# Attention tiles of a four-layer convolution kernel: the order of the two head pairs' score matmuls

## The chip, the cores and the metric

The kernel runs on one core of one Trainium2 chip. The metric is the device time of one execution in microseconds (us); where several runs were made, their median is given. The core's engines run their own instruction streams and wait for each other through semaphores: TensorE (PE, with its weight loads listed apart as PEld), VectorE (DVE), ScalarE (ACT), GpSimd (POOL) and SyncE (SP), which here issues DMAs.

## The reference

The input x is 4 x 256 x 48 x 48. Four layers follow, each adding to x what it computes from the group-normalised x:

```python
x = x + _L0_conv_ref(_gn(x), ...)   # 7x7 dilated conv, softmax over 49 taps, weighted patches
x = x + _L1_conv_ref(_gn(x), ...)   # 3x3 conv, sign weights
x = x + _L2_conv_ref(_gn(x), ...)   # 3x3 conv, ternary weights
x = x + _L3_conv_ref(_gn(x), ...)   # windowed linear attention
```

The change lies in layer 3. With 8 heads of 32 channels:

```python
q = sigmoid(Wq x);  k = sigmoid(Wk x);  v = Wv x / |Wv x|      # per head
for w in (1, 2, 4):                                            # window 48/w
    wk  = box sum of k over the window around each pixel
    wkv = box sum of the outer products k v over the same window
    attn = (q . wkv) / (q . wk + 1e-6)
out = Wout [attn of the three windows] + bout
```

## The kernel before, in words

Layers 0 to 2 come first (in the profiled execution up to 1389 us) and the change does not touch them.

Layer 3 does not form the box sums of k v. It works like masked attention without a softmax: for a block of queries (8 image rows of 48 pixels, of one image and one half of the heads) and a tile of 128 keys (8 rows by 16 columns) it computes the scores k . q, sets those outside the window to zero, and sums v over the keys with the masked scores as weights. `Block` (from line 1826) holds one block of queries; there are 48 blocks (4 images, 2 halves with 4 heads each, 6 row groups) with 15 key tiles on average, 720 tiles in all. A tile's work in TensorE's program is:

- `scores` (line 1837), called once for each pair of heads (`pr` = 0 or 1). It takes a tile of the pool `ps_s`, two PSUM banks, and issues two matmuls of 32 rows by 128 columns, one for each head of the pair. The four heads of a half lie in partitions 0, 32, 64 and 96, so the first pair's matmuls use TensorE's row groups 0 and 32, the second pair's 64 and 96. In f32 each matmul is two passes, and leaves two records in the profile.
- `unseen` (line 1855): one small bf16 matmul for each head, in the same row groups and banks, adds -1024 to scores that the widest window does not see. It goes through the first pair, then the second.
- `masked` (line 1875) is the work of other engines on the banks. In a full tile (all its rows inside the widest window) ACT applies Relu to the second pair, DVE multiplies the first pair by the middle window's mask, then ACT does the first pair and DVE the second. In an edge tile ACT does the first pair and DVE the second, once each. POOL makes the narrowest window's part from the middle's. The results are `sm` tiles in SBUF.
- `sums` (line 1980): matmuls of v (128 rows by 32 columns, a column group for each head) with the `sm` tiles into three accumulators `acc`. The main loop (line 2201) places the sums of a tile two tiles behind its scores (`LAG = 2`), after the scores and penalties of the present tile.

`ps_s` has two tiles, one for each pair, so that a tile's scores start when ACT and DVE have left the banks of the tile before. PSUM is full: four banks of scores, three accumulators and one bank for all other products.

All these engines are wrapped in `InOrder` (line 200): their instructions stay in the order in which Python issues them. Between tiles `advance` (line 302, called at 2229) lets jobs put in a step each: projections of the next image, key sums, norms, window states, the output projection. Their pace is set by an estimate of each tile's mask and sum times; it does not depend on the order of the pairs.

The lines that this document follows are the main loop's call

```python
ss = [blocks[i].scores(pr, a, c) for pr in range(NPR)]
blocks[i].unseen(ss, a, c)
ahead.append(blocks[i].masked(a, c, ss))
```

with NPR = 2, and the two matmul loops in `scores` and `unseen`. Every instruction carries the line of the wrapper, L208, in the profile, so groups are told apart by the names of their tiles: s (scores and penalties), sm, acc.

Of the kernel before, what the change touches and what calls it, by code (L numbers as in the profile page):

```python
# [211 lines left out]
def conv_preact_kernel(  # L212
# [89 lines left out]
    def advance(time=None):  # L302

        nonlocal step, spare
        step += 1
        spare = ALL if time is None else min(spare, 0.0) + time
        for entry in list(active):
            if entry[0] <= step:
                wait = next(entry[1], None)
                if wait is None:  # L310
                    active.remove(entry)
                else:
                    entry[0] = step + wait
# [4 lines left out]
    def until(*keys):  # L318
        while not made.issuperset(keys):
            assert active  # L320
            advance()
# [1246 lines left out]
    with (  # L1568
# [23 lines left out]
        NPR = HG // 2  # L1592
# [406 lines left out]
        def seen(wi, a, rb):  # L1999
            r0, r1 = rows_seen(wi, a, rb)  # L2000
            return r0 < r1
# [128 lines left out]
        def begun(i):  # L2130

            b, ct, rb = order[i]
            if (ct, rb) == (0, 0) and b + 1 < B:
                everything = ("q0", "q1", "k0", "k1", "v")
                following = Projection(b + 1, scr, *bank_m).groups([(a, everything) for a in range(NRB)])
                start(paced(following, 2))
            blocks[i] = Block(b, ct, rb, qs.pop(i))

        def midway(i):

            b, ct, rb = order[i]
            if (b, ct) == (0, 0) and 0 < rb <= NRB - seen_first:
                a = seen_first - 1 + rb
                until(("k", 0, 0, a), ("v", 0, a))
                load_kv(0, 0, a)
            if ct == NCT - 1:
                start(prepare(i))
            if i + 1 < len(order):
                start(window_state(i + 1))
                nb, nct, nrb = order[i + 1]  # L2150
                until(("q", nb, nct, nrb))
                qs[i + 1] = load_q(*order[i + 1])

        def done(i):

            b, ct, rb = order[i]
            finishing.append((i, blocks.pop(i).stage))
            nb, nct = b + (ct + 1) // NCT, (ct + 1) % NCT
            if nb < B:
                for a in LOADS.get(rb, ()):  # L2160
                    until(("k", nb, nct, a), ("v", nb, a))
                    load_kv(nb, nct, a)
# [7 lines left out]
        def mask_time(i, a, c):  # L2170

            rb = order[i][2]

            def elements(wi, cols):
                y0, y1 = rows_seen(wi, a, rb)
                return 2 * (y1 - y0) * (cols[1] - cols[0])

            if not rows_whole(a, rb):
                return 150 + 0.87 * elements(0, cols_seen(0, c))
            on_act = sum(150 + 0.87 * elements(0, cols) for cols in strips(c))  # L2180
            on_dve = (elements(1, cols_seen(1, c)) + 130) / 0.96
            return on_act + on_dve + max(0, max(on_act, on_dve) - min(on_act, on_dve))

        def sums_time(i, a, c, at):

            rb, time = order[i][2], 0
            for wi in range(NW):
                if seen(wi, a, rb):
                    y0, y1 = rows_seen(wi, a, rb)
                    parts = strips(c) if wi == 0 and rows_whole(a, rb) else [cols_seen(wi, c)]  # L2190
                    time += product_time((y1 - y0) * sum(p1 - p0 for p0, p1 in parts))
            if at == 0:
                time += 300
            if at == 6:
                time += product_time(sum(RB * (c1 - c0) for c0, c1 in map(cols_whole, range(NKC))))
            return time

        blocks, ahead = {}, []
        start(window_state(0))
        start(finish_all())  # L2200
        for n in range(len(stream) + LAG):
            if n < len(stream):
                i, a, c, at, last = stream[n]
                if at == 0:
                    begun(i)
                ss = [blocks[i].scores(pr, a, c) for pr in range(NPR)]
                blocks[i].unseen(ss, a, c)
                ahead.append(blocks[i].masked(a, c, ss))
                if at == 5:
                    midway(i)  # L2210
            if n >= LAG:
                i, a, c, at, last = stream[n - LAG]
                sms = ahead.pop(0)
                if at == 0:
                    if i >= 2:
                        until(("done", i - 2))
                    blocks[i].begin()
                if at == 6:
                    until(("window", i))
                    blocks[i].whole(i)  # L2220
                for wi in (1, 0, 2):
                    if seen(wi, a, order[i][2]):
                        blocks[i].sums(wi, a, c, sms)
                if last:
                    done(i)
            time = 1000.0
            if LAG <= n < len(stream):
                time = 900.0 + mask_time(*stream[n][:3]) - sums_time(*stream[n - LAG][:4])
            advance(max(time, 500.0))
# [46 lines left out]
```

## Time and profile before

| what | value |
|---|---|
| median of 3 runs | 3482.7 us (3479.43 to 3486.44) |
| profiled execution: device time, span | 3485.36 us, 3483.6 us |
| granted TensorE clock, mean | 0.951 |
| span before layer 3's tiles, PE busy in it | 1389 us, 1162.9 us |
| span of layer 3's tiles, PE busy in it | 2095 us, 1896.7 us |
| in it, busy on s: PE, PEld | 719.2 us, 264.4 us |
| in it, busy on sm from s: DVE, ACT | 753.0 us, 559.1 us |
| in it, POOL busy (all work) | 1353.8 us |

The page lists an engine's busy time, the chain of work that ended last with its shares of the span, and groups of like instructions: output<-inputs, count, busy time, mean length of one in ns, and the idle time of the engine before them with what ended most of it. An answer on waits reads: who waited for whom, us in total, number of times, longest. A timeline line has the start and the length in us, the engine, the operation, the operands and how many instructions are merged in it; for merged lines the length is from the first start to the last end. Busy time of a group of concurrent matmuls is counted once, while the mean length is that of one.

### The profile page before, as it was taken

What the parts mean: (1) busy time and instruction counts of PE and PEld (TensorE: products, weight loads), DVE (VectorE), ACT (ScalarE), POOL (GpSimd) and SP (SyncE); (2) the same over time, 40 slices, a digit from 0 to 9 for tenths busy, and PEclk for the clock granted to TensorE, in tenths of its full rate; (3) what the DMA queues carried; (4) which work ended last, traced back from release to release, by engine and by line L of the source; (5) the groups of instructions that cost most, each with busy time, mean ns of one, the idle gap of its engine ahead of it and who ended that gap; (6) DMA issues with size and microseconds to landing.
All of it is one profiled execution on the core that took longest, in us unless ns stands there. A gap on an engine that the chain in (4) does not pass through costs nothing.

```text
span 3483.6 us, 78045 instructions
## 1 busy us (share of the span) xinstructions
PE 3059.6 (88%) x31634; PEld 1931.6 (55%) x31634; DVE 1994.0 (57%) x3595; ACT 1041.5 (30%) x2782; POOL 1532.2 (44%) x2548
## 2 busy tenths in 40 slices
PE   3579999999899788888789988889998999989998
PEld 2467776767768557444344544444554444545544
DVE  7986488568657336465564445554456554444444
ACT  0012111211111423444323433433344433334432
POOL 0000030021011214587886678786557786534443
PEclk9799899999999899999899999999999999999999
DMA  7745413413322422344554444354423454401221
GB/s 256 236 139 174 141 63 122 154 54 129 120 94 85 138 89 98 120 132 145 164 144 129 127 137 146 116 158 134 124 81 119 130 150 122 114 29 52 81 63 56
DMA packets 373052, 423.34 MB, mean 122 GB/s; under 512 B 129076, under 2 KB 328532, under 8 KB 371540
## 3 DMA queue, kind: packets, MB, share of 16 engines
q1 hardware_dynamic: 371491, 416.32, 38.3%
q8 instruction: 249, 4.08, 0.5%
q0 software_dynamic: 144, 1.24, 0.2%
q14 instruction: 112, 0.91, 0.1%
q10 hardware_dynamic: 1056, 0.79, 0.1%
HBM read 288.24 MB, written 131.25 MB: 120 GB/s over the span
## 4 chain that ended last, share of the span: by engine, by line
PE 56%; POOL 12%; DVE 11%; ACT 4%; issue 3%; DMA 3%; SPq 1%; ACTq 0%; POOLq 0%; DVEq 0%
PE s L208 15%; PE cv L208 14%; PE acc L208 11%; PE out_ps L208 6%; PE proj_ps L208 4%; DVE sm L208 3%; POOL nhi L208 3%; ACT sm L208 3%; POOL sm L208 3%; POOL pt L208 2%; PE ap L208 2%; POOL vu L208 1%; DVE l2v L208 1%; DVE v L208 1%; DVE k L208 1%
## 5 line engine op out<-in xcount | busy, mean ns | idle before, releaser
L208 DVE TENSOR_TENSOR sm<-s,masks 128x432 f32<-128x432 f32 (+8 forms) x1152 | 634.4, 578 | 627.8 <-PE s L208 582.0
L208 POOL TENSOR_TENSOR sm<-sm,masks 128x336 f32<-128x336 f32 (+8 forms) x768 | 606.1, 809 | 662.6 <-DVE sm L208 656.2
L208 ACT ACTIVATE sm<-s 128x128 f32<-128x128 f32 (+3 forms) x1680 | 559.1, 361 | 1030.9 <-PE s L208 820.9
L208 PE MATMUL s<-qs,ks 32*128 32x320 f32 (+3 forms) x5760 | 664.5, 506 | 127.9 <-DVE sm L208 61.6
L208 PE MATMUL acc<-sm,vs 128*32 128x64 f32 (+13 forms) x14976 | 681.8, 306 | 48.6 <-POOL sm L208 48.5
L208 PE MATMUL cv<-vx,wt 128*128 128x288 f32 x2080 | 560.1, 425 | 93.2 <-DVE vx L208 52.6
L208 PEld LDWEIGHTS acc<-sm,vs 128*32 128x32 f32 x14976 | 347.9, 110 | 384.5 <-issue 258.4
L208 PEld LDWEIGHTS cv<-vx,wt 128*128 128x128 f32 x2080 | 402.5, 198 | 214.5 <-issue 56.7
L208 PEld LDWEIGHTS s<-qs,ks 32*128 32x128 f32 x5760 | 264.4, 187 | 422.9 <-ACT sm L208 172.4
L208 POOL MEMSET v<- 128x16 f32 (+1 forms) x120 | 18.5, 215 | 727.7 <-DVE vx L208 634.5
L208 PE MATMUL cv<-v,wl 128*128 128x384 f32 x1152 | 225.1, 355 | 25.7 <-DVE x L208 10.6
L208 DVE TENSOR_SCALAR sm<-s 128x672 f32<-128x672 f32 (+1 forms) x144 | 118.6, 824 | 202.8 <-PE s L208 198.1
L208 PEld LDWEIGHTS cv<-v,wl 128*128 128x128 f32 x1152 | 214.3, 194 | 36.0 <-issue 15.9
L208 PE MATMUL s<-masks 24*128 24x128 bf16 (+4 forms) x2880 | 217.7, 236 | 0.0
L208 POOL TENSOR_TENSOR pt<-pt 128x144 f32<-128x144 f32 x336 | 188.5, 561 | 23.0
L208 POOL TENSOR_TENSOR v<-l2v,v 128x384 fp32r<-128x384 f32 x96 | 109.0, 1163 | 120.2 <-ACT v L208 111.3
L208 POOL TENSOR_TENSOR nhi<-nhi,nq 128x384 f32<-128x384 f32 x144 | 144.8, 1033 | 0.2
L208 PE MATMUL cv<-pad,wl 128*128 128x384 bf16 x864 | 143.1, 327 | 0.0
L208 PE MATMUL out_ps<-o,wout_sb 128*128 128x384 f32 x288 | 130.2, 534 | 3.6 <-DVE res L208 2.8
L208 PEld LDWEIGHTS <-masks 24*128 24x128 bf16 x2880 | 101.5, 95 | 53.9 <-issue 3.5
L208 PEld LDWEIGHTS <-wl 128*128 128x128 bf16 x864 | 83.8, 97 | 59.3 <-issue 0.7
L208 PE MATMUL out_ps<-stage,wout_sb 128*128 128x384 f32 x288 | 116.4, 486 | 0.0
(176 smaller groups left out, 3568.6 us busy)
## 6 DMA issues: line engine op xcount, KB each, us to landing
wt<-wt SPq DMA_DIRECT2D x48, 768.0 KB
kb_d<-pt SPq DMA_DIRECT2D x48, 576.0 KB
rc<-r_d SPq DMA_DIRECT2D x192, 144.0 KB
nhi<-kb_d SPq DMA_DIRECT2D x120, 192.0 KB
nlo<-kb_d SPq DMA_DIRECT2D x88, 192.0 KB
o_d<-stage SPq DMA_DIRECT2D x24, 576.0 KB
o<-o_d SPq DMA_DIRECT2D x24, 576.0 KB
wl<-wl_d SPq DMA_DIRECT2D x16, 768.0 KB
```

The lines of the kernel that those rows point to most:

```text
L208: return lambda *args, **kwargs: self.tc.keep_in_program_order(op(*args, **kwargs))
```

## The change

The first and the second pair's scores change places in TensorE's program. `reversed(range(NPR))` allocates and computes pair 1 first, then pair 0; the `[::-1]` puts the two tiles back in their old order in `ss`, so that `unseen` and `masked` treat them as before: penalties for pair 0, then pair 1, and the same operations of ACT and DVE on each.

```diff
@@ -2203,7 +2203,7 @@
                 i, a, c, at, last = stream[n]
                 if at == 0:
                     begun(i)
-                ss = [blocks[i].scores(pr, a, c) for pr in range(NPR)]
+                ss = [blocks[i].scores(pr, a, c) for pr in reversed(range(NPR))][::-1]
                 blocks[i].unseen(ss, a, c)
                 ahead.append(blocks[i].masked(a, c, ss))
                 if at == 5:
```

## The prediction

> **What bounds the kernel now.** I read the page first (busy time, chain, groups), then the waits and the chain of layer 3's stretch, then single tiles in the timeline.
>
> ```profile
> PE 3059.6 (88%) x31634; PEld 1931.6 (55%) x31634; DVE 1994.0 (57%) x3595; ACT 1041.5 (30%) x2782; POOL 1532.2 (44%) x2548
> PE s L208 15%; PE cv L208 14%; PE acc L208 11%; PE out_ps L208 6%; PE proj_ps L208 4%; DVE sm L208 3%; POOL nhi L208 3%; ACT sm L208 3%; POOL sm L208 3%; POOL pt L208 2%; PE ap L208 2%; POOL vu L208 1%; DVE l2v L208 1%; DVE v L208 1%; DVE k L208 1%
> L208 PE MATMUL s<-qs,ks 32*128 32x320 f32 (+3 forms) x5760 | 664.5, 506 | 127.9 <-DVE sm L208 61.6
> L208 PE MATMUL s<-masks 24*128 24x128 bf16 (+4 forms) x2880 | 217.7, 236 | 0.0
> ```
>
> TensorE is busy 88% of the span, and the scores (s) are the largest item of the chain that ended last. 5760 score records are 720 tiles of 8: four heads, two passes each. 5760 times 506 ns would be 2915 us, but their busy time is 664.5: the four heads run side by side in four groups of 32 rows. Within layer 3 alone (1389 to 3484 us) the chain's answer gives PE s 25.7% of 2095 us, 538 us, the largest item again. The waits of that stretch:
>
> ```profile
> DVE sm L208 <- PE s L208: 780.1, 617, 11.0
> PE s L208 <- DVE sm L208: 61.6, 92, 9.5
> PE s L208 <- ACT sm L208: 60.4, 110, 4.0
> ```
>
> TensorE itself waits for a released score bank only some 122 us in all. The individual records show 272 of 720 tiles starting after such a gap. So two kinds of tile matter: those where TensorE arrives late anyway (448), and those where the masks of the tile before hold it (272). Two tiles from the timeline:
>
> ```profile
> 2507.91 0.93 PE L208 MATMUL s<-qs,ks 32*128 32x384 f32 x8
> 2508.66 0.24 PE L208 MATMUL s<-masks 24*128 24x128 bf16 x4
> 2508.93 0.81 DVE L208 TENSOR_TENSOR sm<-s,masks 128x624 f32<-128x624 f32 x1 [2.14 <-PE s L208]
> ...
> 2501.47 0.96 PE L208 MATMUL s<-qs,ks 32*128 32x320 f32 x8
> 2502.11 0.38 PE L208 MATMUL s<-masks 24*128 24x128 bf16 x4
> 2502.41 0.75 PEld L208 LDWEIGHTS acc<-sm,vs 128*32 128x32 f32 x24 [0.32 <-issue]
> 2502.49 1.12 DVE L208 TENSOR_TENSOR sm<-s,masks 128x432 f32<-128x432 f32 x2 [0.46 <-PE s L208]
> ```
>
> In the first, all four heads start together. In the second, pair two's bank came free 0.155 us late, so its scores and its penalty matmuls follow by that much: the block of four penalty matmuls is 0.38 long instead of 0.24. Yet DVE, which needs the first pair alone, starts at 2502.49, at the end of the whole block, as in the first tile.
>
> **What the skill says.** The Trainium skill, "TensorE: Matmul & The Clock Gate", Part 3, says that matmuls in different row groups run concurrently and start about 4 ns apart, and that matmuls are strict FIFO in start and end. The trace has the concurrency, at 6.7 ns spacing. On FIFO it is mixed: a head's second pass starts 0.373 us after its first, and the next head's first pass, later in the program, starts after 0.007; if the two passes count as one instruction the rule holds. That DVE waits for the block's end supports ends in order: pair one's completion is reported only after pair two's scores, which stand before it. "TensorEngine Tiling (Array Packing)", Key Properties, says that changing the tiling mode drains the array: here the first sum (128x32) starts 0.145 us after the last 128-column penalty matmul starts and 0.225 to 0.25 after one of 320 to 384 columns, so the last penalty matmul sets when the sums begin.
>
> **The change, part by part.**
>
> 1. Instructions. None is added or removed. In the built program 2880 TensorE instructions change their row position and their bank: per tile the four score matmuls go from row groups 0, 32, 64, 96 to 64, 96, 0, 32. The penalty matmuls stay at 0, 32, 64, 96. No DMA moves, and no instruction of DVE, ACT, POOL or SP.
>
> 2. Waits. Every engine's waits stand at the same places with the same values. The pool hands the slot that is released first to whichever pair is allocated first; so the first two score matmuls still wait for what the first two waited for. The change therefore doesn't let either pair start on another release. Cost nothing; there is no cover to lose.
>
> 3. Pair one's scores start two issue places later: 2 x 6.7 = 13.4 ns where both banks are free. The penalty matmuls begin with its row group 0. The records of an undisturbed tile have the penalties at 0.643, 0.649, 0.656 and 0.663 us after the first score, each as its row group comes free. After the change row group 0 comes free at 0.656; in order the four stand at 0.656, 0.663, 0.669 and 0.676. The block ends 13.4 ns later, and so do the sums and everything behind. 720 x 13.4 ns = 9.6 us at most. Of that, what lies on the path: the blocks from first score to next matmul average 0.935 us, 673 us together, of which the chain holds 538, 80%. 0.80 x 9.6 = 7.7 us.
>
> 4. Tiles where the second place waits longer (232 of 720, 36.9 us in all, median 0.14). Before, pair one's completion was free to run ahead but was reported only when pair two's scores ended: DVE's first mask starts a median 0.256 us after pair one's last penalty matmul in undisturbed tiles, and in disturbed ones at best 0.222 after pair two's last. After, pair one is in the late place and completes 0.256 after its penalties: from 0.885 to 0.919 us past the late start, 34 ns. 20 ns of it are beyond part 3. In full tiles ACT's and DVE's second operations wait for the longer of the two first ones, mostly DVE's 0.6 us against ACT's 0.38, so the release moves by that. 72 full tiles are disturbed and hold the tile behind: 72 x 20 ns = 1.4 us. In edge tiles ACT takes pair one and could lose up to 0.1 us, but DVE's longer operation on pair two (0.82 against 0.70) comes later and the next tile's second place waits for it: nothing, or 20 x 0.1 = 2 us if not so.
>
> Sum: 7.7 + 1.4 = 9.1, taken as 9 us. The profiled execution took 3485.4 us with a span of 3483.6; it becomes 3494.4 and 3492.6. The median of the runs, 3482.7, lies 2.7 below the profiled one: 3491.7. From both ends: part 3 lies between 0 (if penalties overtake each other) and 9.6, part 4 between 0 and 12 (third rival). A gain has no source: no engine can begin anything earlier, since ACT's first operation waits for the last penalty matmul in both orders.
>
> **The rivals.**
>
> *Overtaking, not slower.* If TensorE lets pair two's penalties go ahead as soon as their row groups are free, they stand at 0.643 and 0.649, pair one's at 0.656 and 0.663, and the block ends when it ended before. Part 3 vanishes for the 448 tiles where TensorE is the limit; part 4's 1.4 us and perhaps 1 us through DVE in held tiles stay. About 3485, within the measurement. It decides at one point: whether the third penalty record comes before the first. For it speaks that second passes are overtaken by other heads' first passes; against it, that each head may be one instruction, and the skill's sentence.
>
> *Pair one's whole delay counts.* If pair one's completion had been reported early before, the change would now delay DVE's first mask by the full lateness of the second place. In full tiles that hold the next, this lateness sums to 12.1 us (in those that do not, 16.9, hidden behind sums and projections). 7.7 + 12.1 = 20 us: 3502. Against it: DVE's start follows the end of the block in the second tile shown and in the records generally.
>
> *Hidden altogether.* 20% of the score time is off the chain, where POOL, DMA and projections set the pace. If held tiles and POOL's lateness (PE acc waits 48.5 us for POOL sm) swallow more than that, the result falls toward 3486. I count this with the first rival.
>
> *Phase effects.* Runs of one kernel spread over 7 us, and moving 720 tiles by nanoseconds may shift DMA and clock phases either way, below 3476 too.
>
> **How the numbers follow.** A difference of 0.2% (7 us) is about what a measurement of this kernel can tell from no change. In order, 3487 to 3497: 0.57, of which 0.43 slower by over 0.2% (above 3489.7) and 0.14 within. Overtaking or hidden, 3481 to 3489: 0.25, of which 0.03 slower, 0.21 the same, 0.01 faster. Whole delay, 3497 to 3507: 0.11, nearly all slower (0.11). Phase effects 0.07, faster. Slower 0.57, same 0.35, faster 0.08. The likeliest is 3491.7; for it alone 3487 to 3497. The range takes in the first rival down to 3480 and part of the third up to 3502.
>
> **What would show it.** Right: in an undisturbed tile the four penalty matmuls start about 0.656 to 0.676 us after the first score, still 6.7 ns apart in program order, and the first sum 0.145 after the last; no new waits; TensorE's idle time before s hardly changed; DVE's start in disturbed tiles about 0.03 us later past the late place. Overtaking: the last penalty still at 0.663. Whole delay: TensorE's waits for DVE sm and ACT sm before s grow by several us. Wrong altogether: a stage before 1389 us changes, or the time from first score to penalties grows by tens of ns, a cost of the order of row groups that the trace of before cannot show.

## The result, and the profile after

| | before | after |
|---|---|---|
| median of 22 runs each | 3479.0 us (3470.56 to 3486.44) | 3486.8 us (3479.29 to 3497.73) |
| ratio after to before, 95% interval | | 1.0021 (1.0012 to 1.0030) |
| profiled execution's span | 3483.6 us | 3477.5 us |
| in it, from the first score of layer 3 to the first score of its last tile | 1389.2 to 3461.9: 2072.7 us | 1379.8 to 3455.8: 2076.0 us |

The change makes the kernel slower by 0.21%, 7.3 us of 3479 (interval 4.2 to 10.4; the two medians lie 7.8 apart). That is small against the spread of single runs, 16 to 18 us: the profiled execution of after happens to be shorter than that of before, because layers 0 to 2, which the change doesn't touch, took 9.4 us less in it. Inside layer 3 it is 3.3 us longer. So the two traces are compared tile by tile, not by their spans.

The lines of after's page that answer to those shown of before (busy time, the chain by line, the two groups of s: busy and mean ns, then the idle time before them):

```profile
PE 3055.0 (88%) x31634; PEld 1926.6 (55%) x31634; DVE 1994.7 (57%) x3595; ACT 1043.6 (30%) x2782; POOL 1532.7 (44%) x2548
PE s L208 16%; PE cv L208 14%; PE acc L208 11%; PE out_ps L208 6%; PE proj_ps L208 4%; DVE sm L208 3%; ACT sm L208 3%; POOL nhi L208 3%; POOL sm L208 3%; POOL pt L208 2%; PE ap L208 2%; DVE l2v L208 1%; POOL vu L208 1%; DVE v L208 1%; SPq L208 1%
L208 PE MATMUL s<-qs,ks 32*128 32x320 f32 (+3 forms) x5760 | 664.8, 507 | 133.6 <-ACT sm L208 65.5
L208 PE MATMUL s<-masks 24*128 24x128 bf16 (+4 forms) x2880 | 216.6, 236 | 0.0
```

Scores and penalties are busy as long as before (664.5 and 217.7). Idle time before the scores grew from 127.9 to 133.6, and what ends most of it is now ACT with 65.5; before, DVE (61.6) and ACT (60.4) were nearly even. The waits of layer 3's stretch say the same:

```profile
DVE sm L208 <- PE s L208: 786.5, 616, 11.0
...
PE s L208 <- ACT sm L208: 65.5, 126, 4.0
PE s L208 <- DVE sm L208: 63.3, 93, 9.4
```

DVE waits 6.4 us more for scores (780.1 before), TensorE 5.1 and 1.7 us more for ACT and DVE (60.4 and 61.6). The same two tiles as in the prediction, in the timeline of after:

```profile
2498.01 0.93 PE L208 MATMUL s<-qs,ks 32*128 32x384 f32 x8
2498.76 0.24 PE L208 MATMUL s<-masks 24*128 24x128 bf16 x4
2499.03 0.81 DVE L208 TENSOR_TENSOR sm<-s,masks 128x624 f32<-128x624 f32 x1 [2.14 <-PE s L208]
...
2491.56 0.96 PE L208 MATMUL s<-qs,ks 32*128 32x320 f32 x8
2492.20 0.38 PE L208 MATMUL s<-masks 24*128 24x128 bf16 x4
2492.51 0.92 PE L208 MATMUL acc<-sm,vs 128*32 128x224 f32 x20
2492.62 1.13 DVE L208 TENSOR_TENSOR sm<-s,masks 128x432 f32<-128x432 f32 x2 [0.50 <-PE s L208]
```

In the first nothing moves by more than the 0.01 of these lines. In the second tile the penalty matmuls again begin 0.64 us after the first score and last 0.38, the sums begin 0.95 after the first score as before. Only DVE is later: 1.06 after the first score, 1.03 before. The individual records, which are finer than these lines, have the four penalties at 0.643, 0.649, 0.798 and 0.804 us after the first score. Pair one's scores stand in the late place now and started their second pass only at 0.528 and 0.535, so the two penalties at 0.643 and 0.649 can only be pair two's, which stand behind pair one's in the program. They overtake.

### The profile page after: what moved, and what is told of

Read it like the earlier page. It is cut to its first block, busy times and chain, and to the rows that moved or that the text cites. A ratio compares the mean times of both kernels' runs of the same rounds, so it can differ in the third digit from the quotient of the medians.

```text
span 3477.5 us, 78045 instructions
## 1 busy us (share of the span) xinstructions
PE 3055.0 (88%) x31634; PEld 1926.6 (55%) x31634; DVE 1994.7 (57%) x3595; ACT 1043.6 (30%) x2782; POOL 1532.7 (44%) x2548
## 4 chain that ended last, share of the span: by engine, by line
PE 56%; DVE 11%; POOL 11%; ACT 4%; issue 3%; DMA 3%; SPq 1%; ACTq 0%; POOLq 0%; DVEq 0%
PE s L208 16%; PE cv L208 14%; PE acc L208 11%; PE out_ps L208 6%; PE proj_ps L208 4%; DVE sm L208 3%; ACT sm L208 3%; POOL nhi L208 3%; POOL sm L208 3%; POOL pt L208 2%; PE ap L208 2%; DVE l2v L208 1%; POOL vu L208 1%; DVE v L208 1%; SPq L208 1%
## 5 line engine op out<-in xcount | busy, mean ns | idle before, releaser
L208 PE MATMUL s<-qs,ks 32*128 32x320 f32 (+3 forms) x5760 | 664.8, 507 | 133.6 <-ACT sm L208 65.5
```

Source lines behind the costliest of these rows:

```text
L208: return lambda *args, **kwargs: self.tc.keep_in_program_order(op(*args, **kwargs))
```

## What the starts show, tile by tile

This table is worked out from the individual records. A tile is late (the prediction calls it disturbed) when its second place started later than normal, because that bank came free later; it is held when TensorE stood idle before its first score. Readers are the first operation on pair one (DVE) and on pair two (ACT) in full tiles, in us past the first score plus the second place's lateness, which is what its start lies beyond the normal 0.0135 us; of each group the first quartile, since some operations wait for something else as well. The second part takes the tiles that are held by a bank in the run named and in before, and sums how much later their first and their second place start, measured from the end of TensorE's work before.

```
                        first reader of       first reader of     held tiles, later than before by
                        pair one (DVE)        pair two (ACT)      (sum, us)
                        undisturbed late      undisturbed late    first place   second place
before                  0.905       0.887     1.007       0.988      -             -
after                   0.918       0.919     1.020       1.020      5.9           4.7   (269 tiles)
e1_pens_swapped         0.960       0.960     0.977       0.977     14.7          10.0   (270)
e2_mirror               0.905       0.886     1.007       0.987      0.1           0.2   (271)
e3_by_pair              0.898       0.738     1.034       0.978     -7.3           0.7   (247)
e4_both_swapped         0.947       0.931     0.965       0.946      8.5           3.2   (270)
e5_full_only            0.918       0.919     1.020       1.020      7.8           7.4   (270)
e6_edge_only            0.906       0.887     1.007       0.988      2.5           1.6   (268)
```

In after every first reader of a full tile starts 13 ns later, and 32 ns later where the second place is late. The median of the block from first score to next matmul is 0.889 us in both. Split by the tile in front, the 5.9 us of after are: behind undisturbed full tiles 142 tiles, 1.5 us (median 12 ns); behind disturbed full tiles 70, 2.1 us (32 ns); behind undisturbed edge tiles 37, 0.5 us (14 ns); behind disturbed edge tiles 20, 1.9 us (89 ns; at the second place 0.8 us).

The traces also keep the moments at which a semaphore was raised. Both pairs raise the same one with their last penalty: DVE waits for the earlier of its two counts in before and after, ACT for the later. In undisturbed full tiles at full clock the medians past the first score are 0.882 and 0.924 us in before, 0.895 and 0.937 in after. In both the first count comes 16 to 17 ns behind the profile's end of pair one's last penalty (0.865 in before, 0.879 in after) and the second 42 ns behind the first, though in after pair two's penalties had run first. In the disturbed tile of after that is shown above, pair two's penalties end at 0.865, but no count comes before 1.036, 16 ns after the end of pair one's; the second follows at 1.078. In the same tile of before, pair one's penalties end at 0.865, and the first count comes at 1.004, after pair two's scores (0.962).

## The experiments

Two theories stood against each other after the result. *Order of the scores*: a pair of row groups that is issued in second place costs by itself, on TensorE, whatever stands behind it. *Place of completion*: TensorE loses nothing itself; pair one's completion is reported later, so its first reader and all that follows it start later, and the tiles that are held by a bank pay. All ratios are against runs of before on the same chip.

**e1_pens_swapped**: scores as before, the penalties alone in the other order.

```diff
-                for pr, s in enumerate(ss):
+                for pr, s in reversed(list(enumerate(ss))):
```

> The kernel before with only the penalties' order turned: scores pair one, pair two; penalties pair two, pair one. Theory 'order of the scores' (a pair of row groups that is issued late costs by itself): scores stand as before, so no loss, 3479 within 3 us. Theory 'place of completion' (the loss comes through the first reader of pair one, whose last instruction moved to the end of the block): that instruction is last here too, so the same loss as the change, +5 to +9 us, and DVE's first mask in full tiles starts 0.918 us past the later place, as after the change (0.905 undisturbed and 0.886 disturbed before).

Measured: 1.0035 (1.0017 to 1.0053), 12 us slower. Its waits in layer 3:

```profile
PE s L208 <- ACT sm L208: 79.5, 142, 4.8
```

In before this wait was 60.4, and TensorE's whole idle time before the scores grew from 127.9 to 143.3. The scores stand as before, and the loss is larger than the change's and than expected. So a loss of this kind needs no change in the order of the scores. The reader's start was expected at 0.918 and is 0.960. The disturbed tile of above, in this run's timeline:

```profile
2503.02 0.88 PE L208 MATMUL s<-qs,ks 32*128 32x320 f32 x8
2503.67 0.29 PE L208 MATMUL s<-masks 24*128 24x128 bf16 x4
2504.04 1.12 DVE L208 TENSOR_TENSOR sm<-s,masks 128x432 f32<-128x432 f32 x2 [0.54 <-PE s L208]
2504.06 0.38 ACT L208 ACTIVATE sm<-s 128x256 f32<-128x256 f32 x1 [1.09 <-PE s L208]
```

Its records have penalties at 0.643, 0.649, 0.714 and 0.721. The scores of pair two are the late ones here, so the first two penalties are pair one's: they overtake pair two's, which stand before them, and end at 0.866. The two counts come at 0.953 and 0.995, and DVE, which now waits for the second, starts at 1.018. So pair one is done early, and is reported after pair two all the same. ACT's first operation is 0.030 earlier in the table, and that helps little because DVE's operation is the longer. The sum in held tiles, 10 to 15 us, fits the 12 measured, but 3.5 us of it sit in three single tiles.

**e4_both_swapped**: the change, with the penalties turned in the same way (the edit of e1 on the changed kernel).

> The change with the penalties turned too: scores and penalties pair two, then pair one; readers as before. Theory 'order of the scores' through the issue order of penalties behind scores: the block is in step again, so the time of before. Theory 'place of completion': pair one's last penalty is still the last of the block, so the loss of the change stays, +5 to +9 us, with DVE's first start at 0.918; ACT's first operation in full tiles could start some ns earlier, which hides behind DVE's longer one.

Measured: 1.0018 (1.0008 to 1.0028), 6 us slower, as the place of completion had it. Scores and penalties are in step here, so being out of step is not the cause. DVE's start is at 0.947, later than expected, ACT's at 0.965, earlier than before by 0.042: whichever pair's last penalty comes first in the program is reported first (0.882 in the median), the other 42 ns behind.

**e2_mirror**: the change, and all its readers turned with it.

```diff
-                for pr, s in enumerate(ss):
+                for pr, s in reversed(list(enumerate(ss))):
...
-                pairs = [room() for _ in ss]
+                pairs = [room() for _ in ss][::-1]
...
-                first, second = zip(ss, pairs)
+                second, first = zip(ss, pairs)
...
-                for tiles in pairs:
+                for tiles in reversed(pairs):
...
-                    for j in range(HG):
+                    for j in (2, 3, 0, 1):
```

> The change, with everything behind it turned as well: penalties pair two first, DVE begins with pair two and ACT with pair one in full tiles, ACT takes pair two and DVE pair one in edge tiles, POOL and the sums take pair two first. Row groups 64 and 96 are issued first as in the change. Theory 'order of the scores' in the sense of the row groups themselves: the loss stays, +7 us. Theory 'place of completion': a pure renaming of the pairs, so the time of before, within 3 us, and DVE's first start back at 0.905 and 0.886.

Measured: 1.0003 (0.9991 to 1.0015), and the starts of before to 1 ns. (In the table its pair one is the pair that DVE reads first.) Row groups 64 and 96 in front cost nothing that this measurement shows (upper end 5 us). Scores and penalties stand in TensorE's program exactly as in e4, which lost 6 us; only what reads them, and the sums behind, is turned. What costs is that the pair whose reader is the longer one, DVE's, is not the pair that is reported first.

**e3_by_pair**: the kernel before, with each pair's penalties directly behind its scores.

```diff
-                ss = [blocks[i].scores(pr, a, c) for pr in range(NPR)]
-                blocks[i].unseen(ss, a, c)
+                ss = [None] * NPR
+                for pr in range(NPR):
+                    ss[pr] = blocks[i].scores(pr, a, c)
+                    blocks[i].unseen([(pr, ss[pr])], a, c)
...
-                for pr, s in enumerate(ss):
+                for pr, s in ss:
```

> The kernel before with each pair's penalties directly behind its scores: pair one's scores and penalties, then pair two's. Theory 'place of completion' with penalties that are overtaken: pair one is reported before pair two's scores end, DVE's first mask starts 0.905 us past the first place even where the second is late, and the tile behind is released earlier where DVE's first operation is the longer one: 3 to 8 us faster than before. If TensorE holds its program at pair one's penalties until their row groups are free, pair two's scores start some 0.35 to 0.6 us late in every tile: over 200 us slower.

Measured: 0.9997 (0.9985 to 1.0009); no gain, and no hundreds of us lost. The disturbed tile of above, in this run's timeline:

```profile
2499.65 0.99 PE L208 MATMUL s<-qs,ks 32*128 32x320 f32 x8
2500.29 0.41 PE L208 MATMUL s<-masks 24*128 24x128 bf16 x4
2500.55 1.27 DVE L208 TENSOR_TENSOR sm<-s,masks 128x432 f32<-128x432 f32 x2 [0.30 <-PE s L208]
```

DVE starts at 2500.55, before the penalties end at 2500.70. In this tile of before and after it started only at or behind that end. This shows what the prediction had argued: in the old order pair one's completion is held until pair two's scores, which stand in front of its penalties, are done. It also shows overtaking a second time: pair two's scores, behind pair one's penalties in the program, start 0.020 us after pair one's in an undisturbed tile, long before those penalties (0.642). The gain was expected to be 3 to 8 us and isn't there: the held tiles' first place comes 7.3 us earlier in sum, their second place 0.7 later. ACT's start on pair two is 0.027 later in undisturbed tiles. Pair two's scores now start at 0.020 in place of 0.0135, which makes the block of an undisturbed full tile 7 ns longer in the median; over 720 tiles that would be 5 us by estimate. And the second place's release is what TensorE's block ends on. Which of these took the gain no run separates.

**e5_full_only and e6_edge_only**: the change in full tiles alone, and in edge tiles alone.

```diff
-                ss = [blocks[i].scores(pr, a, c) for pr in range(NPR)]
+                swap = -1 if rows_whole(a, order[i][2]) else 1
+                ss = [blocks[i].scores(pr, a, c) for pr in range(NPR)[::swap]][::swap]
```

(e6 has `not rows_whole`.)

> The change in full tiles alone (576 of 720); edge tiles keep the old order. Theory 'place of completion': the first readers in full tiles start 13 ns later (undisturbed) and 32 ns later (disturbed), and 215 of the 272 held tiles stand behind a full tile: 143 x 0.013 + 72 x 0.032 = 4 us slower, 2 to 6; readers in edge tiles as before. Theory that the loss sits in the edge tiles, where ACT's start in disturbed tiles moved by 0.11 us: within 2 us of before.

> The change in edge tiles alone (144 of 720). Theory 'place of completion' with full tiles as the main place: 57 held tiles stand behind an edge tile, 37 x 0.013 + 20 x 0.013 to 0.11 = 0.7 to 2.7 us slower, not to be told from nothing. Theory that the loss sits in the edge tiles: +5 to +8 us.

Measured: 1.0007 (0.9996 to 1.0019) and 1.0003 (0.9991 to 1.0014), 2.4 and 1.0 us. Both intervals hold the expected values of the place of completion and also nothing; a loss of 5 to 8 us in edge tiles alone is just excluded by e6 (upper end 4.9). The two losses add up to 3.4 us, less than half of the change's 7.3, but with intervals this wide that is no contradiction, and it doesn't show how the loss is divided. In the traces each moves its own tiles alone. Of the 7.8 us in e5's held tiles 4.5 sit in three single tiles, 3.3 in the rest, which is near the 3.6 of full tiles in after; e6's 2.5 is near after's 2.4.

**e8_edge_roles**: before, with DVE on pair one and ACT on pair two in edge tiles.

```diff
-                    widest(act, *first)
-                    widest(dve, *second)
+                    widest(dve, *first)
+                    widest(act, *second)
```

> The kernel before, with the two operations of edge tiles exchanged: DVE takes pair one, ACT pair two. DVE's operation is the longer (0.82 against 0.70 us) and now starts on the pair that is reported first. Theory 'place of completion': both end about 1.75 us after the first score in place of 1.68 and 1.84, the second place of the tile behind is free some 0.09 us earlier; 57 held tiles, so 2 to 5 us faster. If what counts is only the first place's release: 57 x 0.07 = 4 us slower.

Measured: 1.0003 (0.9989 to 1.0017). The gain of 2 to 5 us that was expected is not in the time, though what should bring it is in the trace: behind edge tiles the second place starts 2.0 us earlier in sum and the first 7.0 later, behind full tiles the second place 1.5 later. At the second place that is nearly nothing in sum. That the first place's 7.0 us cost nothing fits that the second place's release counts.

**e9_edge_roles_changed_order**: the same edit on the changed kernel.

> The change, with the two operations of edge tiles exchanged in the same way: DVE takes pair one, which is now in the late place, ACT pair two. Theory 'place of completion': no better than the change, +5 to +10 us against before, since pair one is reported last of the scores and the gain of the exchange in edge tiles (2 to 5 us) is taken back by full tiles. Theory that the order of the scores doesn't matter once the edge roles fit: the time of the kernel before or better.

Measured: 1.0019 (1.0009 to 1.0028), 6.6 us slower, as the place of completion had it. In held tiles the second place starts 3.7 us later in sum: 4.3 later behind full tiles, some 0.5 earlier behind edge tiles.

No version beat the kernel before in measured time.

One rival was not separated by any of these experiments: the clock that TensorE was granted. Its mean is on record for each run. Among the 45 and the 51 runs of before that the experiments were compared with, a mean lower by 0.001 goes with 2.3 and 2.5 us more. These runs average 0.9505 and 0.9506, the 22 runs of after 0.9489. By that slope the difference of 0.0016 stands for some 4 us, about half of the measured loss. e1, e4 and e9 lie at 0.9487 to 0.9488 too, but so does e8 with 0.9484, which lost nothing; e2 has 0.9510, e3 and e5 0.9502, e6 0.9495. Whether the later releases bring the lower clock about, or the two came together by chance, no run shows. An estimate for equal clock, with one slope of 2.3 us per 0.001 fitted to all these runs, leaves after 1.8 to 2.4 us slower than before, e1 7.3, e4 1.5, e5 2.3, e6 0.7 and e9 2.2 slower, e2 0.5 slower, e3 1.1 and e8 3.5 faster, each with a standard error of 0.7 to 1.0. (It takes these runs of before for after too.) The losses of the change, e1, e4 and e9 keep their direction at equal clock; their size is in doubt, and e8's expected gain may be there after all.

## Why the prediction was right or wrong

The time was right: 9 us slower forecast, 7.3 measured, interval 4.2 to 10.4. (The forecast of 3491.7 started from the 3482.7 of three runs; with 22 runs before stands at 3479.0, so the differences are what can be compared.) Most of its sum was not, and that the number came out near is luck: a term of 7.7 us that isn't there stood in for terms that were put too low.

*Step 2, waits*: right. Their places didn't move, and 269 of the 272 held tiles are held after as well.

*Step 3, 7.7 us, pair one's two issue places lengthen every block*: wrong. It rested on penalties that go in order. They don't: an undisturbed tile's penalties stand at 0.643 to 0.663 in after as in before, and the block's median is 0.889 in both. This was the first rival's mechanism, and the point named for deciding it, whether a penalty of pair two starts before pair one's, decided for it. The Trainium skill's sentence that matmuls are strict FIFO in start and end ("TensorE: Matmul & The Clock Gate", Part 3) doesn't hold for starts across row groups here. For what is reported to other engines the order of the program does hold: ACT's start on pair two came 13 ns later though its penalties now run 13 ns earlier.

*Step 4, disturbed tiles*: right in mechanism and nearly exact in size for one tile (34 ns forecast, 32 measured), mis-sized in sum. It counted 20 ns of it over 72 full tiles, 1.4 us, because step 3 was thought to hold the other 13. With step 3 gone, the held tiles pay the whole: 1.5 us behind undisturbed full tiles, 2.1 behind disturbed, 0.5 and 1.9 behind edge tiles. The edge tiles' up to 0.1 us was taken as nothing, since the second place would not move; behind disturbed edge tiles the first place paid 1.9 us, close to the bound of 2, and the second, which is the one that counts by e3 and e8, 0.8. Together 5.9 us at the first place, 4.7 at the second, where the first rival had written about 2.4.

*The first rival's time*, 3485, some 2.4 us above the median it started from, was therefore too low: its own mechanism costs about twice as much in the held tiles. *The third rival*, pair one's whole delay, is excluded: late tiles moved by 32 ns, not by their lateness of a median 0.14 us, and e3 shows why. *Phase effects* are not excluded: the lower mean clock of after's runs (0.9489 against 0.9505) is of that kind.

The held tiles start 4.7 to 5.9 us later in sum, which is of the size of the measured 7.3 (from 4.2). How much of it reaches the end of the kernel is not shown: waits behind it can swallow some, and the clock may hold about half of the loss. In the two profiles layer 3 is only 3.3 us longer, though after's had 14 us more at half clock in it (166.5 us against 152.7 by their clock records). Blocks less their lateness sum to 2.2 us more in after's profile, but their median change is 0.000, so that is a few single tiles. What the experiments do show is where the loss comes from: it is there when pair one is reported later (e1, e4, the change) and not to be seen when its readers are turned along (e2).

## What to carry to other kernels

When an order of concurrent matmuls is changed, ask first which of them is reported last, and who waits for it: TensorE's own time may not move at all while every reader starts a few ns later, and here only the tiles that waited for a released bank paid. Put first the operand whose reader is on the longer chain, and turn the readers along with the producers if you must turn one (e2). A price that is multiplied by a count of instructions should be checked on the one assumption that makes it per instruction, here that the queue goes in order. And where a loss is this small, compare the granted clock of the runs before the whole of it is put down to the change.

## What the runs showed of the hardware

- Matmuls in different row groups start out of program order: pair two's penalties at 0.643 us while pair one's, which stand before them, start at 0.798 (after, disturbed tile); pair two's scores at 0.020 while pair one's penalties in front of them start at 0.642 (e3). In e1's disturbed tile pair one's penalties start at 0.643, pair two's, which stand before them, at 0.714.
- Their completion is reported in program order. A penalty that was done early is reported behind the one before it in the program (pair two's, ended at 0.865, counted at 1.078 in after; pair one's, ended at 0.866, counted at 0.995 in e1; both in the disturbed tile), and one is held by earlier matmuls of other row groups (DVE's start in late tiles 0.887 past the late place in before, 0.738 in e3).
- Being reported second costs a reader 42 ns where both pairs are done: the two counts are 42 to 43 ns apart in before, after, e1, e2 and e4. With the 13 ns of a later first count that gives the shifts of e1, +55 ns for DVE and -30 for ACT.
- A mean granted clock lower by 0.001 goes with 2.3 to 2.5 us more in the runs of before.
